# Two heads' scores in two neighbouring PSUM banks under one maximum, with one bank for the up products

## The chip, the cores and the metric

The kernel runs on one core of a Trainium2 chip. The metric is the device time of one execution in microseconds; the median of the runs counts. TensorE (PE) multiplies and transposes into PSUM, which has eight banks of 2 KB per partition; one bank holds one 128x512 float32 result. VectorE (DVE) and ScalarE (ACT) read PSUM, GpSimd (POOL) works in SBUF, and SyncE (SP) issues the DMAs.

## The reference, cut to what matters

Four batches of 512 tokens with 512 features go through four gated layers, each added to its input: a WKV recurrence over time, an FFN with ternary weights and int8 groups, a cross attention with 16 heads, and a ternary linear layer. The change touches the attention and the FFN:

```python
# attention (x is layer-normed; H = 16 heads of Dh = 32)
q = _qdq(x) @ _qdq(wq).T + bq
k, v = jnp.split(cond @ wkv.T + bkv, 2, axis=-1)
attn = jax.nn.softmax(jnp.einsum('bnhd,bmhd->bhnm', q, k) * scale, axis=-1)
o = jnp.einsum('bhnm,bmhd->bnhd', attn, v).reshape(B, N, C)
out = _qdq(o) @ _qdq(wp).T + bp
# FFN (2048 hidden features)
h = jax.nn.silu(_bitlinear(x, w1)) * _bitlinear(x, w2)
return _bitlinear(h, w3)
```

## The kernel before

The four batches are pipelined by hand. Each layer of each batch is a generator; `line(gen, *parts)` gives its steps places on a common axis, where one unit is one FFN and `SLOTS` = 17 slots make one unit; `run(until)` always advances the generator whose next step has the smallest place. Each step is a turn: `in_turn` adds an ordering edge behind the last matmul of the turn before, so PE's order is the order of the turns. The order on the other engines is the tile scheduler's.

After a start-up part (weights, keys and values, WKV and FFN of batch 0) comes what I call the grid: the attention of batch b runs beside the FFN of batch b+1, and for half of each FFN beside the WKV scan of batch b+2 as well. Behind the last FFN the attention of batch 2 is finished, and the attention of batch 3 runs without an FFN (`alone`).

An FFN has 16 units (4 token tiles by 4 blocks of hidden features), of four steps each: an up product of eight matmuls into a bank with tag "hp" (`up`, tile ff_hp), read by a tanh on ACT (L745) and a multiply on DVE (`gate`, L746); the down product of the unit two before (ff_acc, tag "acc"); the second up product, read by one DVE instruction (`gated`, L750) and quantised; and the transposes of the quantised product of the unit before (`gate_parts`, tile tp_ps).

The attention has 16 units as well, of two heads (index i) and two token tiles (index t) each, and two more turns to drain. A unit's four steps, interleaved with those of an FFN unit, are: scores for t = 0; the product with the values of the unit two before (`values`, o_ps) and transposes of the weights of the unit before (`turned`, pt_ps, copied by ACT at L970); scores for t = 1; more transposes, the collection of the results (`collect`), and the fetches on SP's queue. One call of `scores(k, i, t)` makes one matmul into a bank with tag "hp" (s_ps, 128x512), one DVE reduction that gives the negated maximum of each row (at_nm, L948), and one exponential on ACT with that maximum as bias and the row sum as accumulated output (at_P, L950).

PSUM has one pool from the end of the start-up on: three banks with tag "m" (all transposes and projections), three with "hp" (scores and up products), two with "acc". A tile takes a free buffer of its tag; the first instruction that writes a new tile waits until all readers of the buffer's last tile are done.

The functions that the diff touches, and what calls them:

Of the kernel before, what the change touches and what calls it, by code (L numbers as in the profile page):

```python
# [10 lines left out]
F32 = mybir.dt.float32  # L11
# [5 lines left out]
ALU = mybir.AluOpType  # L17
AX = mybir.AxisListType
PSUM = bass.MemoryType.PSUM
DRAM = bass.MemoryType.DRAM  # L20

P = 128
# [8 lines left out]
def kernel(  # L31
# [36 lines left out]
    nc = tc.nc  # L68
    NB, T, D = x.shape
# [11 lines left out]
    sm = ctx.enter_context(tc.tile_pool(name="small", bufs=4))  # L81
# [3 lines left out]
    psum = {}  # L85
# [41 lines left out]
    def psum_tile(name, tag, dtype=F32):  # L127
        pool, bufs = psum["now"]
        return pool.tile([P, D], dtype, name=name, tag=tag, bufs=bufs[tag])
# [17 lines left out]
    def in_turn(ins):  # L147


        if "on" in turn:  # L150
            if "ahead" in turn:
                behind(ins, turn["ahead"])
            turn["last"] = ins
        return ins

    def next_turn():

        if "last" in turn:
            turn["ahead"] = turn["last"]

    def matmul(*args, **kwargs):
        return in_turn(nc.tensor.matmul(*args, **kwargs))  # L162
# [677 lines left out]
    def attention_layer(b, xb, pool, tiles=range(NT)):  # L840
# [41 lines left out]
        qR, kR, V, PT, sums, made, lanes, out_s = {}, {}, {}, {}, {}, {}, {}, {}  # L882
# [38 lines left out]
        def fetch_keys(p):  # L921
            kR[p] = pool.tile([P, 2, T], F32R, name="at_kR", tag="at_kR")
            stack(kR[p], kD[b][p // 2][:, pair(p), :], (0, 1, 0, 1))
# [10 lines left out]

        units = [(p, h) for p in range(NP) for h in range(len(tiles) // 2)]

        def scores(k, i, t):

            p, h = units[k]
            if k not in sums:  # L940
                sums[k] = sm.tile([P, 2, 2], F32, name="at_sum", tag="at_sum")
            at = t * P
            sp = psum_tile("s_ps", "hp")
            matmul(
                sp, lhsT=qR[k][:, i, at : at + P], rhs=kR[p][:, i, :], start=True, stop=True
            )
            nm = sm.tile([P, 1], F32, name="at_nm", tag="at_nm", bufs=8)
            nc.vector.tensor_reduce(nm, sp, AX.X, ALU.max, negate=True)  # L948
            lanes[k, i, t] = pool.tile([P, T], F32, name="at_P", tag="at_P", bufs=6)
            nc.scalar.activation(  # L950
                lanes[k, i, t],
                sp,
                AF.Exp,
                bias=nm,
                accum_out=sums[k][:, t, i : i + 1],
            )

        def turned(k, i, t):

            if k not in PT:  # L960
                PT[k] = pool.tile([P, 2, NT, 2 * P], F32, name="at_PT", tag="at_PT", bufs=1)
            w = lanes.pop((k, i, t))
            pt = psum_tile("pt_ps", "acc" if alone else "m")
            for m in range(NT):
                transpose(pt[:, m * P : (m + 1) * P], w[:, m * P : (m + 1) * P], ident)
            dst = PT[k][:, i, :, t * P : (t + 1) * P]
            if alone and i:
                made[k] = nc.vector.tensor_copy(dst, blocks(pt))
            else:
                made[k] = nc.scalar.copy(dst, blocks(pt))  # L970

        def values(k):


            p, h = units[k]
            acc = bank("o_ps")[:, 0:P]
            for m in range(NT):
                for i in range(2):
                    for t in range(2):
                        mm = matmul(  # L980
                            acc[rows(2 * i + t), :],
                            lhsT=V[p // 2][:, m, rows(2 * (p % 2) + i)],
                            rhs=PT[k][:, i, m, t * P : (t + 1) * P],
                            start=(m == 0),
                            stop=(m == NT - 1),
                        )
                        behind(mm, made[k])
            del PT[k]
            out_s[k] = pool.tile([P, P], F32, name="at_os", tag="at_os", bufs=1)
            nc.scalar.copy(out_s[k], acc)  # L990
# [71 lines left out]
        for k in range(len(units) + 2):  # L1062
            now, before = k < len(units), 0 < k <= len(units)
            if k > 1 and not alone:
                turned(k - 2, 1, 1)
            for i in range(2):
                if now:
                    scores(k, i, 0)
            yield
            if k > 1:  # L1070
                values(k - 2)
            next_turn()
            for i in range(1 + alone):
                if before:
                    turned(k - 1, i, 0)
            if alone and k > len(units):
                next_turn()
                next(ahead)
            yield
            if before and not alone:  # L1080
                turned(k - 1, 1, 0)
            for i in range(2):
                if now:
                    scores(k, i, 1)
            yield
            for i in range(1 + alone):
                if before:
                    turned(k - 1, i, 1)
            next_turn()
            if k > 1:  # L1090
                collect(k - 2)
            if now:
                p, h = units[k]
                if h == 0:
                    if p + 1 < NP:
                        fetch_keys(p + 1)
                    if p % 2 == 0 and p // 2 + 2 < NC:
                        next_turn()
                        project(p // 2 + 2)
                elif p % 2 and p // 2 + 1 < NC:  # L1100
                    fetch_values(p // 2 + 1)
                if k + 2 < len(units):
                    fetch_queries(k + 2)
            yield
# [90 lines left out]
    def place(line):  # L1195

        k = line["step"]
        for start, end, steps in line["parts"]:
            if k < steps:
                at = start + (end - start) * k / steps  # L1200

                return (math.floor(at * SLOTS) + 0.8) / SLOTS if line["aside"] else at
            k -= steps
        return end

    def run(until):
        while lines:
            now = min(lines, key=place)
            if place(now) > until:
                return  # L1210
            try:
                next(now["gen"])
                now["step"] += 1
                next_turn()
            except StopIteration:
                lines.remove(now)

    lines = []

    SLOTS = NT * NF + 1  # L1220

    def line(gen, *parts, aside=False):
        lines.append({"gen": gen, "parts": parts, "step": 0, "aside": aside})

    xs = {}
    with (
# [108 lines left out]
        for b in (2, 3):  # L1335
            line(
                next_batch(b),
                (b - 1.0 - 4.2 / SLOTS, b - 1.0 - 4.2 / SLOTS, 1),
                (b - 1.0 - 3.2 / SLOTS, b - 1.0 - 3.2 / SLOTS, 1),
                (b - 1.0 + 1.8 / SLOTS, b - 1.0 + 5.8 / SLOTS, 4),  # L1340
                (b - 1.0 + 5.05 / SLOTS, b - 1.0 + 13.05 / SLOTS, 32),
            )
        run(0.99)
    nc.sync.dma_start(out=gamma_b, in_=bcast(gamma))
    ps = ctx.enter_context(tc.tile_pool(name="ps", bufs=1, space=PSUM))
    psum["now"] = ps, {"m": 3, "hp": 3, "acc": 2}
    at = ctx.enter_context(tc.tile_pool(name="att", bufs=2))
    for b in range(NB):
        if b:
            early = (0.99, 1.0, 4) if b == 1 else (b - 0.19, b - 0.1, 3), (b - 0.08, b, 1)  # L1350
            line(
                late(lambda b=b: ffn_layer(xs[b])),
                *((early[0],) if b == 1 else early),
                (b, b + 16 / SLOTS, 64),
                (b + 16 / SLOTS, b + 17.75 / SLOTS, 7),
            )
        start = b + 1 + 4.95 / SLOTS
        end = start + 18 / SLOTS
        line(
            late(lambda b=b: attention_layer(b, xs[b], at)),  # L1360
            (b + 1.0 if b == 0 else b + 0.7, b + 1.03 if b == 0 else b + 0.9, 5),
            (b + 1 + 1.7 / SLOTS, b + 1 + 3.7 / SLOTS, 5),
            (b + 1 + 3.75 / SLOTS, b + 1 + 4.35 / SLOTS, 2),
            (start, end, 72),
            (end, end + 2.4 / SLOTS, 6)
            if b != NB - 2
            else (end - 0.15 / SLOTS, end + 4.65 / SLOTS, 6),
            (end + 2.4 / SLOTS, end + 3.4 / SLOTS, 4),
        )
        if b < NB - 1:  # L1370
            line(
                late(lambda b=b: ternary_layer(b, xs[b], at)),
                (end + 3 / SLOTS, end + 8 / SLOTS, 8)
                if b < NB - 2
                else (end + 4.85 / SLOTS, end + 11.85 / SLOTS, 7),
                aside=b < NB - 2,
            )
    run(NB + 9)


# [43 lines left out]
```

## Time and profile before

| what | value |
|---|---|
| median of 3 runs | 1094.46 us (1093.98 to 1096.87) |
| profiled execution | 1094.21 us |
| span of its instructions | 1092.4 us |
| busy PE, DVE, ACT, POOL | 943.3, 827.0, 729.9, 320.7 us |
| granted TensorE clock, mean | 0.956 |
| scores: matmuls, maxima, exponentials | 256 of each |
| up products | 128, of 8 matmuls each |

Times in the lines are microseconds, "mean ns" is the duration of one instruction. "Idle before" is the time in which an engine stood still ahead of an instruction, and "<-" names what ended it. PEld are weight loads, which overlap matmuls. In timelines "x2" means that two neighbouring instructions are merged into one line.

### The profile page before, as it was taken

Reading aid. Unit: us, or ns where it says so; the run is one execution under the profiler, and the core shown is the slowest. Engines: PE = TensorE matmul, PEld = TensorE weight load, DVE = VectorE, ACT = ScalarE, POOL = GpSimd, SP = SyncE. Lnnn points to the kernel's source line nnn. Section 1 sums busy time; section 2 is a strip of 40 time slices with the busy share of each in tenths; the row PEclk is TensorE's granted clock in tenths of the full one; section 3 lists DMA queues with packets and bytes.
Section 4 is the critical chain, followed back from the end, with each engine's and each line's share of the span. In section 5 each row is a group of like instructions: output and inputs, shape, how many; then the busy total and the mean of one; then the engine's idle time right before and its main releaser. Section 6 shows DMA issues by size and latency. Waiting matters only on the chain.

```text
span 1092.4 us, 17928 instructions
## 1 busy us (share of the span) xinstructions
PE 943.3 (86%) x6350; PEld 680.0 (62%) x6380; DVE 827.0 (76%) x1600; ACT 729.9 (67%) x1490; POOL 320.7 (29%) x328
## 2 busy tenths in 40 slices
PE   3879997998879888799997886999999999878975
PEld 2345564565557666677775665677776777655652
DVE  5985548757876899896769898966687866579976
ACT  5656755567545776667877576677685777877863
POOL 3831104423333254621215545412122410100000
PEclk8889999999999999999999798999999999989998
DMA  8188845464445674645576354655574563244311
GB/s 288 39 272 317 323 169 190 144 221 155 154 146 181 221 234 127 231 129 169 185 234 204 121 177 133 204 195 180 184 231 156 184 210 116 59 148 116 116 42 39
DMA packets 85674, 189.68 MB, mean 174 GB/s; under 512 B 12241, under 2 KB 36817, under 8 KB 74577
## 3 DMA queue, kind: packets, MB, share of 16 engines
q1 hardware_dynamic: 85584, 188.53, 51.7%
q8 instruction: 51, 0.84, 0.3%
q14 instruction: 39, 0.31, 0.1%
HBM read 148.65 MB, written 39.85 MB: 173 GB/s over the span
## 4 chain that ended last, share of the span: by engine, by line
PE 49%; DVE 22%; ACT 14%; POOL 5%; issue 5%; DMA 4%; SPq 1%; ACTq 0%; POOLq 0%; DVEq 0%
PE ff_hp L162 15%; PE pt_ps L165 7%; PE ff_acc L162 6%; PE o_ps L162 4%; PE v_ps L162 4%; PE s_ps L162 3%; ACT at_P L950 3%; DVE wk_q L640 3%; ACT at_PT L970 3%; DVE at_nm L948 2%; PE k_ps L162 2%; DVE wk_p L634 1%; PE qr_ps L165 1%; PE tp_ps L165 1%; ACT wk_e L612 1%
## 5 line engine op out<-in xcount | busy, mean ns | idle before, releaser
L162 PE MATMUL ff_hp<-wT,xp 128*128 128x512 f32 x1024 | 275.7, 412 | 6.6 <-DVE ff_z L746 3.7
L162 PEld LDWEIGHTS ff_hp<-wT,xp 128*128 128x128 f32 x1024 | 195.4, 196 | 54.6 <-DVE ff_z L746 5.7
L950 ACT ACTIVATE at_P<-s_ps,at_nm 128x512 f32<-128x512 f32 x256 | 175.0, 690 | 45.2 <-DVE at_nm L948 43.4
L948 DVE TENSOR_REDUCE at_nm<-s_ps 128x1 f32<-128x512 f32 x256 | 166.6, 677 | 38.4 <-PE s_ps L162 37.9
L970 ACT COPY at_PT<-pt_ps 128x512 f32<-128x512 f32 x224 | 131.2, 590 | 72.6 <-PE pt_ps L165 71.9
L685 POOL TENSOR_TENSOR ff_z<-qg_b,qg_s 128x512 f32<-128x512 bf16 x64 | 71.9, 1124 | 314.6 <-ACT qg_b L684 304.7
L165 PE MATMUL pt_ps<-ident,at_P 128*128 128x128 f32 x1024 | 155.4, 280 | 9.0 <-ACT at_PT L970 4.3
L165 PEld LDWEIGHTS pt_ps<-ident,at_P 128*128 128x128 f32 x1024 | 118.1, 142 | 47.3 <-ACT at_PT L970 10.9
L162 PE MATMUL ff_acc<-wT,hr 128*128 128x512 f32 x512 | 137.6, 409 | 5.2 <-DVE hr L697 2.6
L162 PE MATMUL s_ps<-at_kR,at_qR 128*128 128x512 f32 x256 | 103.0, 464 | 24.0 <-ACT at_P L950 17.6
L162 PEld LDWEIGHTS ff_acc<-wT,hr 128*128 128x128 f32 x512 | 92.9, 191 | 26.2 <-DVE hr L697 4.2
L162 PE MATMUL o_ps<-at_PT,at_V 128*32 128x128 f32 x2048 | 75.4, 281 | 4.7 <-ACT at_PT L970 2.8
L162 PEld LDWEIGHTS o_ps<-at_PT,at_V 128*32 128x32 f32 x2048 | 54.8, 111 | 28.6 <-issue 11.6
L746 DVE SCALAR_TENSOR_TENSOR ff_z<-ff_z,ff_hp 128x512 f32<-128x512 f32 x64 | 43.4, 679 | 37.0 <-ACT ff_z L745 36.9
L745 ACT ACTIVATE ff_z<-ff_hp,coef 128x512 f32<-128x512 f32 x64 | 44.1, 688 | 40.5 <-PE ff_hp L162 38.1
L750 DVE SCALAR_TENSOR_TENSOR ff_z<-ff_hp,coef,ff_z 128x512 f32<-128x512 f32 x64 | 47.7, 745 | 30.2 <-PE ff_hp L162 30.1
L684 ACT CAST qg_b<-qg_i 128x512 bf16<-128x512 int8 x80 | 49.3, 617 | 27.4 <-DVE qg_i L680 17.3
L162 PEld LDWEIGHTS s_ps<-at_kR,at_qR 128*128 128x128 f32 x256 | 43.3, 194 | 36.4 <-ACT at_P L950 25.2
L162 PE MATMUL v_ps<-wkvT,cT 128*128 128x512 f32 x128 | 60.5, 618 | 5.5 <-DVE wT L303 2.3
L162 PE MATMUL k_ps<-cT,wkvT 128*128 128x512 f32 x128 | 61.3, 631 | 2.3 <-ACT wk_k L584 1.0
L640 DVE RECIPROCAL wk_q<-wk_q 128x256 f32<-128x256 f32 x32 | 54.5, 1722 | 3.0 <-POOL wk_q L635 1.6
L696 ACT CAST hr<-tp_ps 128x512 fp32r<-128x512 f32 x64 | 37.6, 588 | 21.7 <-PE tp_ps L165 21.7
(180 smaller groups left out, 1669.4 us busy)
## 6 DMA issues: line engine op xcount, KB each, us to landing
wT<-wD SPq DMA_DIRECT2D x72, 1024.0 KB, 5.4
wn<-in_L_ffn_w_dram SPq DMA_DIRECT2D x18, 1024.0 KB, 6.2
at_kR<-kD SPq DMA_DIRECT2D x128, 128.0 KB, 4.0
at_qR<-qD SPq DMA_DIRECT2D x256, 64.0 KB, 2.5
wD<-wT SPq DMA_DIRECT2D x12, 1024.0 KB, 4.2
kD<-k_half SPq DMA_DIRECT2D x16, 512.0 KB, 2.8
qD<-at_half SPq DMA_DIRECT2D x32, 256.0 KB, 2.2
cn<-in_ctx_dram SPq DMA_DIRECT2D x8, 512.0 KB, 5.9
```

Of the source, the lines that this page charges most:

```text
L162: return in_turn(nc.tensor.matmul(*args, **kwargs))
L165: return in_turn(nc.tensor.transpose(*args))
L640: nc.vector.reciprocal(half, half)
L684: nc.scalar.copy(qb, qi)
L685: nc.gpsimd.tensor_tensor(grouped(src), grouped(qb), s.unsqueeze(2).to_broadcast([P, NG, GS]), ALU.mult)
L696: nc.scalar.copy(part[:, 0, :], pt)
L745: nc.scalar.activation(z, hp, AF.Tanh, scale=coef[:, 0:1])
L746: nc.vector.scalar_tensor_tensor(z, z, 1.0, hp, ALU.add, ALU.mult)
L750: nc.vector.scalar_tensor_tensor(z, hp, coef[:, 1:2], z, ALU.mult, ALU.mult)
L948: nc.vector.tensor_reduce(nm, sp, AX.X, ALU.max, negate=True)
L950: nc.scalar.activation(lanes[k, i, t], sp, AF.Exp, bias=nm, accum_out=sums[k][:, t, i : i + 1],)
L970: made[k] = nc.scalar.copy(dst, blocks(pt))
```

## The change

In the grid, the two heads' scores of one token tile go into one PSUM tile of two neighbouring banks (tag "pair", one buffer). One DVE reduction gives both maxima (128x2), and the two exponentials follow. The tag "hp" keeps one bank, which only the up products use in the grid. The pool is closed one slot behind the last FFN, `SWAP` = 1/17 of a unit, and a new pool with the layout of before is opened; from then on scores are made one at a time as before. The start-up part is not touched.

```diff
+        def weighed(k, i, t, sp, nm):
+
             lanes[k, i, t] = pool.tile([P, T], F32, name="at_P", tag="at_P", bufs=6)
             nc.scalar.activation(
                 lanes[k, i, t],
...
-        def scores(k, i, t):
+        def scores(k, t):
 
             p, h = units[k]
             if k not in sums:
                 sums[k] = sm.tile([P, 2, 2], F32, name="at_sum", tag="at_sum")
+            cut = slice(t * P, (t + 1) * P)
+            if "pair" not in psum["now"][1]:
+                for i in range(2):
+                    sp = psum_tile("s_ps", "hp")
+                    matmul(sp, lhsT=qR[k][:, i, cut], rhs=kR[p][:, i, :], start=True, stop=True)
+                    nm = sm.tile([P, 1], F32, name="at_nm", tag="at_nm1", bufs=8)
+                    nc.vector.tensor_reduce(nm, sp, AX.X, ALU.max, negate=True)
+                    weighed(k, i, t, sp, nm)
+                return
+            ps_pool, bufs = psum["now"]
+            sp = ps_pool.tile([P, 2, T], F32, name="s_ps", tag="pair", bufs=bufs["pair"])
+            for i in range(2):
+                matmul(
+                    sp[:, i, :], lhsT=qR[k][:, i, cut], rhs=kR[p][:, i, :], start=True, stop=True
+                )
+            nm = sm.tile([P, 2], F32, name="at_nm", tag="at_nm", bufs=4)
+            nc.vector.tensor_reduce(nm, sp, AX.X, ALU.max, negate=True)
+            for i in range(2):
+                weighed(k, i, t, sp[:, i, :], nm[:, i : i + 1])
...
-            for i in range(2):
-                if now:
-                    scores(k, i, 0)
+            if now:
+                scores(k, 0)
...
-            for i in range(2):
-                if now:
-                    scores(k, i, 1)
+            if now:
+                scores(k, 1)
...
+    SWAP = 1.0 / SLOTS
...
-    ps = ctx.enter_context(tc.tile_pool(name="ps", bufs=1, space=PSUM))
-    psum["now"] = ps, {"m": 3, "hp": 3, "acc": 2}
+    stage = ctx.enter_context(ExitStack())
+    ps = stage.enter_context(tc.tile_pool(name="ps", bufs=1, space=PSUM))
+    psum["now"] = ps, {"m": 3, "hp": 1, "acc": 2, "pair": 1}
...
+    run(NB + SWAP)
+    stage.close()
+    ps = ctx.enter_context(tc.tile_pool(name="ps_end", bufs=1, space=PSUM))
+    psum["now"] = ps, {"m": 3, "hp": 3, "acc": 2}
     run(NB + 9)
```

More of the change, by code (lines that the diff above doesn't have):

```diff
@@ L935, in attention_layer @@
         units = [(p, h) for p in range(NP) for h in range(len(tiles) // 2)]
-        def scores(k, i, t):
[L939 to L948, printed above, removed]
+        def weighed(k, i, t, sp, nm):
             lanes[k, i, t] = pool.tile([P, T], F32, name="at_P", tag="at_P", bufs=6)
@@ L956, in scores @@
             )
+        def scores(k, t):
+            p, h = units[k]
+            if k not in sums:
+                sums[k] = sm.tile([P, 2, 2], F32, name="at_sum", tag="at_sum")
+            cut = slice(t * P, (t + 1) * P)
[17 more added lines that the diff above has]
+                weighed(k, i, t, sp[:, i, :], nm[:, i : i + 1])
         def turned(k, i, t):
```

## The prediction

> **What bounds the kernel now.** I read the page first: PE is busy 86% of the span, DVE 76%, ACT 67%, and the chain that ended last is 49% PE, 22% DVE and 14% ACT. No engine holds the end alone, so I asked for the windows, cut where the grid changes its character. Columns: window, its length, busy time of PE, PEld, DVE, ACT, POOL with instructions, granted clock, DMA share, GB/s.
>
> ```profile
> 365.00:500.00 135.00, 117.59 (x829) 91.28 (x832) 123.44 (x220) 96.56 (x205) 58.45 (x59) 0.96 0.55 175
> 500.00:570.00 70.00, 67.75 (x553) 53.39 (x555) 48.31 (x108) 52.98 (x117) 14.12 (x15) 1.00 0.59 204
> 570.00:690.00 120.00, 95.57 (x636) 72.33 (x633) 106.78 (x186) 80.15 (x161) 63.99 (x61) 0.90 0.52 170
> 690.00:800.00 110.00, 106.39 (x837) 82.81 (x842) 79.50 (x183) 80.42 (x178) 22.47 (x22) 1.00 0.57 186
> ```
>
> The grid (attention of batch b beside the FFN of batch b+1, 365 to 918 us) has two kinds of stretch. Where the WKV scan of a later batch runs too (365 to 500, 570 to 690) DVE is busy 91% and 89% and PE only 87% and 80%: DVE leads. Elsewhere (500 to 570, 690 to 918) PE is busy 96.5% and DVE about 72%: PE leads, and each tenth of a microsecond that PE waits is paid.
>
> Then the costliest groups, for the prices (count, busy us, mean ns, idle before and its releaser):
>
> ```profile
> L950 ACT ACTIVATE at_P<-s_ps,at_nm 128x512 f32<-128x512 f32 x256 | 175.0, 690 | 45.2 <-DVE at_nm L948 43.4
> L948 DVE TENSOR_REDUCE at_nm<-s_ps 128x1 f32<-128x512 f32 x256 | 166.6, 677 | 38.4 <-PE s_ps L162 37.9
> L222 DVE TENSOR_REDUCE w_am<-wn 128x2 f32<-128x1024 f32 x4 | 4.8, 1203 | 3.7 <-DMA wn<-in_L_xattn_wq_dram 3.7
> ```
>
> The third row is the form that the change will issue (two maxima over 2 x 512), though from SBUF. Last, the timeline of one undisturbed unit (start, duration, instruction, idle before):
>
> ```profile
> 519.12 0.71 PE L162 MATMUL s_ps<-at_kR,at_qR 128*128 128x512 f32 x2
> ...
> 519.64 1.29 DVE L948 TENSOR_REDUCE at_nm<-s_ps 128x1 f32<-128x512 f32 x2
> ...
> 520.37 0.69 ACT L950 ACTIVATE at_P<-s_ps,at_nm 128x512 f32<-128x512 f32 x1 [0.38 <-DVE at_nm L948]
> ...
> 521.05 0.68 ACT L950 ACTIVATE at_P<-s_ps,at_nm 128x512 f32<-128x512 f32 x1
> ...
> 522.42 0.72 PE L162 MATMUL s_ps<-at_kR,at_qR 128*128 128x512 f32 x2
> ...
> 522.98 2.00 PE L162 MATMUL ff_hp<-wT,xp 128*128 128x512 f32 x8
> ...
> 525.24 0.68 ACT L745 ACTIVATE ff_z<-ff_hp,coef 128x512 f32<-128x512 f32 x1
> ...
> 526.03 0.69 DVE L746 SCALAR_TENSOR_TENSOR ff_z<-ff_z,ff_hp 128x512 f32<-128x512 f32 x1 [0.52 <-ACT ff_z L745]
> ...
> 527.32 2.01 PE L162 MATMUL ff_hp<-wT,xp 128*128 128x512 f32 x8
> ```
>
> The reader is to see two chains that return to PE: scores, maximum, exponential, next scores; and up product, tanh, multiply, next up product.
>
> **Up products with one bank.** Here the second up product starts at 527.32, after the multiply at 526.03 has let go of the first one's bank (526.72): in the grid the two do not overlap now. I went through all units of the grid: from the 19th unit of the four FFNs (340 us) on, no up product starts before the one ahead of it has been read. Tag "hp" has three buffers and six takers per unit (two scores, an up product, two scores, an up product), so an up product meets the same buffer again and the scores have the other two. The change writes down what the rotation already does, and costs nothing there; the cover is the down product, the values and the transposes that PE has between (up 0 ends 524.98, up 1 starts 527.32). The exception is the first units of batch 1's FFN, before its attention starts. There the second up product starts at 333.66 while the multiply ends at 334.92, the next at 335.57 against 336.52, the next at 337.38 against 339.01: waits of 1.26, 0.95 and 1.63 us, 3.8 together. PE was 90% busy there, so some comes back in later gaps: bounds 0 and 3.8, I take **+2**, the middle.
>
> The Trainium skill ("Perfetto Trace Analysis", section Optimizing Tensor Performance) speaks against one bank: independent matmul groups should rotate through different banks so that reading one overlaps the next group. By the rule every up product would wait for its reading (here 524.98 to 526.72, 1.74 us; 96 of them would be some 167 us); by the row the rotation has stopped overlapping already, and the sum keeps the row.
>
> **One maximum over two banks.** Per pair, two reductions of 677 ns become one of about 1203: 0.15 us of DVE less. If two that stand back to back are the measure (1.29 us above) it is 0.09. The new layout holds until just behind the last FFN: 64 pairs of batches 0 and 1 and 27 of batch 2, 91 in all, so 8.2 to 13.7 us of DVE. Only where DVE leads can it shorten the run: 36 pairs lie in those two windows, 3.2 to 5.4 us; I take **-4.5**, nearer to the row of the same form. Where PE leads, DVE idles anyway. No DMA and nothing on SP or POOL is moved.
>
> **Two exponentials behind one maximum.** Before, the first exponential starts while DVE does the second maximum; the second exponential ends 0.80 us after that maximum (520.93 to 521.73). Now both come behind it: 0.11 for the signal and 0.69 and 0.68, 1.48. So the banks come free 0.68 us later, less the 0.09 to 0.15 that DVE saves: about 0.55; and 0.3 more where DVE stood idle for the second matmul. Queued behind the exponentials on ACT are the tanh, the casts and the copies of the transposed weights.
>
> **One pair buffer.** The next pair's first matmul must now wait for both exponentials, not for one. In the undisturbed unit it starts 0.69 us after the second (521.73 to 522.42), which covers the 0.55 barely. Over the 50 pairs in the stretches that PE leads I compared that matmul's start with the second exponential's end: it comes earlier or less than 0.3 us later eight times (511.64 against 513.21, 530.07 against 530.08, 724.80 against 725.63, 736.74 against 738.28, 755.13 against 755.15, 803.99 against 804.35, 835.35 against 835.88, 865.94 against 865.69). In some of them the second matmul waited already, so what is new is one matmul (0.31) and the 0.55: between 0.2 and 1.4 each, 0.75 in the mean: **+6**, bounds 2 and 11. Where DVE leads the same happens twelve times more, but PE has slack; I take nothing, and up to 36 x 0.5 = 18 us for the upper bound, if the chain of pairs becomes the bound there.
>
> **The tanh behind the exponentials.** Three up products in PE's stretches start 0.05 to 0.61 us after their multiply (752.39, 804.83, 866.57); a tanh that is 0.55 later moves them: **+1.5**, bounds 0 and 2.
>
> **The new PSUM layout.** The pool is closed and opened again once, beside the last batch's start. The profile has one such change, from the start-up pool to this one, near 326 us: there PE stood still 1.30 and 0.72 us in front of the first transposes. If new tiles wait until everything in the old pool is read, PE drains once: **+1.5**, bounds 0 and 4 (one chain of matmul, maximum, two exponentials and the next weights).
>
> **Sum.** 2 - 4.5 + 6 + 1.5 + 1.5 = +6.5 us. The profiled execution took 1094.2 (its span 1092.4 and 1.8 around it), so 1100.7; the median of the runs is 0.25 above it: **1101**. A measurement of this kernel can tell about 0.3%, 3.3 us, from no change.
>
> The skill's same page (Optimizing Scalar/DVE Operations) says both things: larger operations help where the engine is saturated, and breaking them up helps where DVE or ACT is not saturated but makes PE wait. It gives about 125 ns per DVE instruction on PSUM; an estimate by it is 91 x 0.125 = 11.4 us of DVE, inside the bounds above.
>
> **The rivals.**
> *Faster: the DVE time comes through.* If DVE is what the grid waits for even where PE looks full, and a single reduction spares the pairs whose second maximum now stands far behind the first (376.83 and 383.47, with 1.23 and 1.78 us of WKV between), the saving is up to 13.7 and the waits are covered: 1081 to 1091, middle 1087. For it: the chain gives DVE 22%, and 35.8 us of ACT idle in the grid end with this maximum. Against: PE at 96.5% over half the grid. It decides if the waits that I price at 9.5 are below 1.
> *No change.* The buffers were divided so already, and savings and waits cancel: 1094.5 within 3.3.
> *Much slower: the pair's chain becomes the bound where DVE leads.* A 1.2 us reduction behind a WKV reciprocal of 1.7 us holds both banks; 18 us on top of the rest: 1112 to 1125. For it: PE waits up to 2.2 us for these exponentials there. Against: two turns of about 3.6 us each (0.7 + 1.2 + 1.4 and signals) in a unit of some 12 us.
>
> **How the numbers follow.** Forecast (1098 to 1112) 0.45; faster 0.27; no change 0.16; much slower 0.12. Slower is 0.45 + 0.12 = 0.57. The range for 8 in 10 takes the upper two thirds of the faster case and the lower third of the much slower one: 1084 to 1117. The forecast's own range is 1098 to 1112.
>
> **What would show it.** Right: the reduction with 128x2 near 1.2 us, 91 times; DVE busy 8 to 14 us less; PE's waits for the exponentials in the grid above the present 8.5 us; a gap of 1 to 3 us near the second layout; the 500 to 570 stretch a little longer and the 365 to 500 stretch a little shorter. Wrong: PE's waits unchanged, or the 690 to 800 stretch shorter, or up products waiting for their bank all through the grid.

## The result, and the profile after

The kernel became slower: 1124.12 us (median of 4 runs, 1123.95 to 1124.5) against 1094.39 (4 runs, 1093.98 to 1096.87) on the same chip, ratio 1.0267 [1.0249, 1.0285]. Slower was the likeliest forecast, but with 6.6 us in place of 29.7, and the time lies above the range.

The profiled execution after has a span of 1122.2 us, 29.8 more than before, at nearly the same mean granted clock (0.955 against 0.956). PE is busy 946.0 us (before 943.3), DVE 828.9 (827.0), ACT 726.1 (729.9). So no engine has got much more to do; PE stands still 27.1 us longer. The groups say in front of what (count, busy us, mean ns, idle before and its releasers). PE's rows before:

```profile
L162 PE MATMUL ff_hp<-wT,xp 128*128 128x512 f32 x1024 | 275.7, 412 | 6.6 <-DVE ff_z L746 3.7 <-ACT at_P L950 2.1 <-DVE xp L697 0.7
...
L162 PE MATMUL s_ps<-at_kR,at_qR 128*128 128x512 f32 x256 | 103.0, 464 | 24.0 <-ACT at_P L950 17.6 <-DMA at_qR<-qD 4.2 <-DVE ff_z L746 1.8
```

and the rows after:

```profile
L162 PE MATMUL ff_hp<-wT,xp 128*128 128x512 f32 x1024 | 277.4, 413 | 13.8 <-DVE ff_z L746 11.9 <-DVE ff_z L750 1.3 <-DVE xp L697 0.7
...
L940 ACT ACTIVATE at_P<-s_ps,at_nm 128x512 f32<-128x512 f32 x256 | 174.6, 689 | 68.4 <-DVE at_nm L969 57.8 <-DVE at_nm L959 5.4 <-DVE at_s L226 3.6
...
L969 DVE TENSOR_REDUCE at_nm<-s_ps 128x2 f32<-128x1024 f32 x91 | 110.0, 1209 | 36.4 <-PE s_ps L162 36.1
L162 PE MATMUL s_ps<-at_kR,at_qR 128*128 128x512 f32 x256 | 100.0, 460 | 44.5 <-ACT at_P L940 40.7 <-DMA at_qR<-qD 3.8
```

PE's idle time was 24.0 us ahead of the scores (17.6 of it released by an exponential) and 6.6 ahead of the up products. Now it is 44.5 (40.7) and 13.8: 20.5 + 7.2 = 27.7 us more, where PE's whole idle time grew by 27.1; the other rows changed by little together. The scores' wait for the exponentials is the largest part. The merged reduction takes 1209 ns, 91 times; ACT stands still 57.8 us for it and 5.4 for the single ones that remain, where the single ones of before made it wait 43.4.

To see where it arose, I took the start of the first up product of chosen units (of the 64 that four FFNs have, numbered from 0) in both traces, and the start and end of batch 3's attention; each row is the growth of the difference in that stretch, in us. The other columns are experiments described below, each against the profile before.

| stretch | after | e6 | e5 | e8 | e10 |
|---|---|---|---|---|---|
| first units of batch 1's FFN | 4.1 | 4.2 | 4.1 | 4.1 | 0.4 |
| units 21 to 31, DVE leads | 7.1 | 2.1 | 4.2 | 9.0 | 1.0 |
| between the FFNs of batches 1 and 2 | 3.4 | 0.6 | 3.2 | 3.8 | 2.8 |
| units 32 to 47, DVE leads in the first part | 3.3 | 0.1 | -1.2 | -1.8 | 2.1 |
| between the FFNs of batches 2 and 3 | 3.2 | 1.0 | 2.6 | 3.0 | 2.0 |
| units 48 to 63, PE leads | 4.4 | 1.1 | 4.7 | 5.1 | 6.0 |
| behind the last up products, to batch 3's first scores | 5.7 | 2.9 | 7.3 | 8.1 | 5.4 |
| the rest | -1.4 | 0.8 | 0.4 | -0.5 | -1.0 |
| span | 29.8 | 12.8 | 25.3 | 30.8 | 18.7 |

A wide loss, then, in seven places. Some views show its kinds. First the start, in the timeline after (start, duration, engine, instruction, idle before):

```profile
334.48 2.11 PE L162 MATMUL ff_hp<-wT,xp 128*128 128x512 f32 x8 [1.07 <-DVE ff_z L746]
...
337.43 2.14 PE L162 MATMUL ff_hp<-wT,xp 128*128 128x512 f32 x8 [0.84 <-DVE ff_z L750]
...
341.28 2.12 PE L162 MATMUL ff_hp<-wT,xp 128*128 128x512 f32 x8 [1.72 <-DVE ff_z L746]
```

Three up products wait for the reader of the one ahead, as the prediction had it. Next, windows cut at the same up products: before, from unit 21 to unit 31 and from there to unit 32 (window, length, busy PE, PEld, DVE, ACT, POOL, clock, DMA share, GB/s),

```profile
365.63:494.50 128.87, 111.56 (x773) 86.49 (x774) 117.61 (x207) 90.92 (x193) 57.82 (x58) 0.96 0.57 179
494.50:513.36 18.86, 17.83 (x152) 13.70 (x150) 15.37 (x33) 14.86 (x36) 3.63 (x3) 1.00 0.45 157
```

and after:

```profile
369.47:505.39 135.92, 112.40 (x773) 87.51 (x774) 116.09 (x185) 89.92 (x194) 58.27 (x58) 0.95 0.55 172
505.39:527.62 22.23, 17.91 (x151) 13.91 (x150) 16.01 (x30) 15.64 (x36) 3.13 (x3) 1.00 0.53 183
```

In the first pair of lines DVE does save 1.5 us, but its share falls from 91% to 85%: it stands still 8.6 us longer. In the second pair PE does the same 17.9 us of work in 3.4 us more. The waits of PE in the first stretch (total us, times, longest), before,

```profile
PE s_ps L162 <- ACT at_P L950: 6.5, 4, 2.2
PE ff_hp L162 <- DVE ff_z L746: 3.7, 1, 3.7
...
PE ff_acc L162 <- DVE hr L697: 1.0, 2, 0.6
```

and after,

```profile
PE s_ps L162 <- ACT at_P L940: 9.7, 5, 2.7
PE ff_hp L162 <- DVE ff_z L746: 5.5, 3, 2.6
PE ff_acc L162 <- DVE hr L697: 3.1, 2, 1.9
```

show that the loss there is spread: scores 3.2 more, up products 1.8, down products 2.1. My reading, which no run tests, is that where scores start late, what DVE does behind them is late as well. The second stretch is the slot between two FFNs. There PE has no up product to put between two pairs; in the timeline after:

```profile
522.53 0.73 PE L162 MATMUL s_ps<-at_kR,at_qR 128*128 128x512 f32 x2
...
523.12 0.69 DVE L191 BATCH_NORM_STATS2 s<-xb 128x6 f32<-128x512 f32 x1
...
523.74 1.21 DVE L969 TENSOR_REDUCE at_nm<-s_ps 128x2 f32<-128x1024 f32 x1
...
525.07 0.59 ACT L985 COPY at_PT<-pt_ps 128x512 f32<-128x512 f32 x1 [0.20 <-PE pt_ps L165]
...
525.55 0.69 ACT L940 ACTIVATE at_P<-s_ps,at_nm 128x512 f32<-128x512 f32 x1
...
527.05 0.73 PE L162 MATMUL s_ps<-at_kR,at_qR 128*128 128x512 f32 x2 [2.02 <-ACT at_P L940]
```

From scores to scores this is 4.52 us: the maximum ended at 524.95, a copy held ACT until 525.66, and PE stood still 2.02 us. The same slot before:

```profile
510.18 0.71 PE L162 MATMUL s_ps<-at_kR,at_qR 128*128 128x512 f32 x2
...
510.70 1.29 DVE L948 TENSOR_REDUCE at_nm<-s_ps 128x1 f32<-128x512 f32 x2
...
511.64 0.47 PE L162 MATMUL s_ps<-at_kR,at_qR 128*128 128x512 f32 x1
...
511.85 0.69 ACT L950 ACTIVATE at_P<-s_ps,at_nm 128x512 f32<-128x512 f32 x1
...
512.76 0.68 DVE L191 BATCH_NORM_STATS2 s<-xb 128x6 f32<-128x512 f32 x1
```

The next pair's first scores came 1.46 us behind these: with no up product in the slot, the scores had all three "hp" banks. The order on the other engines was also different. Before, the statistic (512.76), a cast (513.19) and a copy (513.65) stood behind this pair's maxima and exponentials; after, all three stand ahead of them. So the change does not only make instructions wait, it also makes the scheduler order them anew: of ACT's 1198 instructions (accumulator reads left out) 93 stand in another order in the trace after, of DVE's 1344 without the maxima 145.

Last, the end. Behind the last up products the first product with the values in the new pool waits for the last exponential of the old one, in the timeline after:

```profile
966.51 1.72 PE L162 MATMUL o_ps<-at_PT,at_V 128*32 128x128 f32 x28 [4.35 <-ACT at_P L940]
```

### The profile page after: what moved, and what is told of

It reads as the page before. It is cut to its first block, busy times and chain, and to the rows that moved or that the text cites. A ratio compares the mean times of both kernels' runs of the same rounds, so it can differ in the third digit from the quotient of the medians.

```text
span 1122.2 us, 17891 instructions
## 1 busy us (share of the span) xinstructions
PE 946.0 (84%) x6350; PEld 683.1 (61%) x6380; DVE 828.9 (74%) x1509; ACT 726.1 (65%) x1490; POOL 321.9 (29%) x328
## 5 line engine op out<-in xcount | busy, mean ns | idle before, releaser
L162 PE MATMUL ff_hp<-wT,xp 128*128 128x512 f32 x1024 | 277.4, 413 | 13.8 <-DVE ff_z L746 11.9
L940 ACT ACTIVATE at_P<-s_ps,at_nm 128x512 f32<-128x512 f32 x256 | 174.6, 689 | 68.4 <-DVE at_nm L969 57.8
L162 PE MATMUL s_ps<-at_kR,at_qR 128*128 128x512 f32 x256 | 100.0, 460 | 44.5 <-ACT at_P L940 40.7
L969 DVE TENSOR_REDUCE at_nm<-s_ps 128x2 f32<-128x1024 f32 x91 | 110.0, 1209 | 36.4 <-PE s_ps L162 36.1
L162 PEld LDWEIGHTS o_ps<-at_PT,at_V 128*32 128x32 f32 x2048 | 54.5, 111 | 30.8 <-issue 13.1
L750 DVE SCALAR_TENSOR_TENSOR ff_z<-ff_hp,coef,ff_z 128x512 f32<-128x512 f32 x64 | 47.7, 745 | 33.0 <-PE ff_hp L162 32.8
L959 DVE TENSOR_REDUCE at_nm<-s_ps 128x1 f32<-128x512 f32 x74 | 48.4, 682 | 13.9 <-PE s_ps L162 13.7
```

The lines of the kernel that those rows point to most:

```text
L750: nc.vector.scalar_tensor_tensor(z, hp, coef[:, 1:2], z, ALU.mult, ALU.mult)
L940: nc.scalar.activation(lanes[k, i, t], sp, AF.Exp, bias=nm, accum_out=sums[k][:, t, i : i + 1],)
```

## The experiments

"Before" was run on the same chip beside each; e10, e13 and e14 ran on another chip than the rest (before 1094.09 us there).

**e1: the division alone.** Single banks and single maxima, divided between the uses as after.

```diff
-    psum["now"] = ps, {"m": 3, "hp": 1, "acc": 2, "pair": 1}
+    psum["now"] = ps, {"m": 3, "hp": 1, "acc": 2, "s": 2}
-                    sp = psum_tile("s_ps", "hp")
+                    sp = psum_tile("s_ps", "s" if "s" in psum["now"][1] else "hp")
```

> The changed kernel's division of the banks (up products one, scores two, with the second layout behind the last FFN), but the scores in single banks, each with its own maximum, as before. Theory T1 (what costs is that the two banks of a pair come free together, only behind the second exponential): most of the 30 us comes back, 1097 to 1104, that is +3 for the second layout and up to +6 for the first units of batch 1's FFN. Rival T2 (the fixed division costs: up products and scores can no longer borrow each other's bank): 1110 to 1124, with the WKV stretch 365 to 500 us and the ends of the FFNs as long as in the changed kernel. My own reading of the trace after: +4 at the first units of batch 1's FFN stays whichever theory holds.

1099.81 us (10 runs, 1094.75 to 1103.9) against 1094.9, ratio 1.0044 [1.0026, 1.0062]: 4.9 us. Its profiled execution was the quickest of the ten, so its trace understates that; it shows 4.1 in the first units of batch 1's FFN, 2.6 behind the last up products, and up to 3.4 less in other stretches. Its times go with the granted clock: 1094.75 and 1095.36 us at 0.966, 1103.73 and 1103.9 at 0.952. In its groups the scores' wait for exponentials is near that before (17.6):

```profile
L162 PE MATMUL s_ps<-at_kR,at_qR 128*128 128x512 f32 x256 | 103.5, 463 | 26.0 <-ACT at_P L940 20.9 <-DMA at_qR<-qD 4.7
```

So the loss is not the division of the banks; some 25 us come with the pair.

**e2: the pair's tile with two maxima.**

```diff
-            nm = sm.tile([P, 2], F32, name="at_nm", tag="at_nm", bufs=4)
-            nc.vector.tensor_reduce(nm, sp, AX.X, ALU.max, negate=True)
             for i in range(2):
-                weighed(k, i, t, sp[:, i, :], nm[:, i : i + 1])
+                nm = sm.tile([P, 1], F32, name="at_nm", tag="at_nm1", bufs=8)
+                nc.vector.tensor_reduce(nm, sp[:, i, :], AX.X, ALU.max, negate=True)
+                weighed(k, i, t, sp[:, i, :], nm)
```

> The changed kernel with its pair tile of two banks, but with two reductions of 512 in place of one of 1024, so that the first exponential can start as early as before. T1 (banks released together): stays slow, 1117 to 1127, since the tile is still free only behind the second exponential. Rival T3 (one late maximum delays the first exponential and all that is queued on ACT behind it): 1100 to 1110. In DVE time: 91 x 0.15 = 14 us more than the changed kernel.

1143.21 us (1138.72 to 1146.52, 4 runs), ratio 1.0431 [1.0403, 1.046]: slower than after by 19, and above both expectations. The group of e2's maxima, and then its timeline, say why:

```profile
L970 DVE TENSOR_REDUCE at_nm<-s_ps 128x1 f32<-128x512 f32 x182 | 123.9, 681 | 76.5 <-PE s_ps L162 43.9 <-ACT at_P L940 31.6
```

```profile
519.29 0.69 ACT L940 ACTIVATE at_P<-s_ps,at_nm 128x512 f32<-128x512 f32 x1 [1.08 <-DVE at_nm L970]
...
520.10 0.69 DVE L970 TENSOR_REDUCE at_nm<-s_ps 128x1 f32<-128x512 f32 x1 [0.84 <-ACT at_P L940]
```

The second maximum starts when the first exponential has ended, though it reads another bank: in this program two engines take turns on one tile. So e2 put in a wait of its own and did not measure lateness; e5 to e8 replace it with single tiles and explicit waits.

**e3: the new pool alone.** After's program, with the layout of before on both sides of the new pool, so that scores are single all through.

```diff
-    psum["now"] = ps, {"m": 3, "hp": 1, "acc": 2, "pair": 1}
+    psum["now"] = ps, {"m": 3, "hp": 3, "acc": 2}
```

> The kernel before with nothing but the closing and opening of the pool one slot behind the last FFN, the same layout (3, 3, 2) on both sides. T4 (the new pool waits until the old one is read): 1097 to 1099, +3 to +4.4 as the trace after shows at 969.86 us against 936.60 before. If tiles only wait for the tiles whose place they take: 1094.4, no difference within 3.

1094.13 us (10 runs, 1092.02 to 1098.71), ratio 0.9995 [0.9981, 1.0008]. Closing and opening the pool costs nothing that the medians can show. Its profile has 2.0 us in the stretch behind the last up products, and -2.3 over all others. The 2.0 have their place in its timeline, where after has its 4.35:

```profile
934.57 1.41 PE L162 MATMUL o_ps<-at_PT,at_V 128*32 128x128 f32 x32 [2.00 <-ACT at_P L940]
```

Before waits for no exponential ahead of such a product, but 1.58 us for one ahead of the next scores (940.11); e1 and e7 wait 1.59 in e3's place, e6 2.03, e5 3.90 and e8 4.40. So the new pool does hold PE, longer where the exponentials are late.

**e4: a second bank for the up products,** taken from the transposes.

```diff
-    psum["now"] = ps, {"m": 3, "hp": 1, "acc": 2, "pair": 1}
+    psum["now"] = ps, {"m": 2, "hp": 2, "acc": 2, "pair": 1}
```

> The changed kernel with two banks for the up products and two instead of three for the transposes and projections. If the single up bank is a main cost (T2's half): the first units of batch 1's FFN lose no 4 us and the WKV stretch shortens by 5 or more, 1108 to 1116, less what the missing transpose bank costs. T1: the pair tile still holds, 1116 to 1126. If the third transpose bank matters more than either: over 1126.

1158.88 us (1157.42 to 1161.16, 4 runs), ratio 1.0579 [1.0563, 1.0595]: 35 us slower than after. The start's loss is gone (0.5 in place of 4.1 up to its third unit), so the one bank was its cause. But two banks for the transposes are too few. A wait of e4 (total us, times, longest):

```profile
PEld tp_ps L165 <- issue: 38.5, 51, 2.3
```

After has 12.3 us in this row.

**e5, e6, e8: the two properties of a pair, one at a time.** On e1's banks, `awaits` adds a wait of one instruction for another. In e5 the first maximum waits for the second matmul and the first exponential for the second maximum: both exponentials are late, but each bank is still released by its own. In e6 nothing is late, but the first matmul of the next pair waits for the second exponential. e8 has both, so it is the change with two reductions in place of one.

```diff
+                for i in range(2):
+                    sps.append(psum_tile("s_ps", "s" if split else "hp"))
+                    mms.append(
+                        matmul(sps[i], lhsT=qR[k][:, i, cut], rhs=kR[p][:, i, :], start=True, stop=True)
+                    )
+                if split and "e" in last_exp:
+                    awaits(mms[0], last_exp["e"])          # e6, e8
+                for i in range(2):
...
+                    reds.append(nc.vector.tensor_reduce(nms[i], sps[i], AX.X, ALU.max, negate=True))
+                if split:
+                    awaits(reds[0], mms[1])                # e5, e8
                 for i in range(2):
+                    e = weighed(k, i, t, sps[i], nms[i])
+                    if split and i == 0:
+                        awaits(e, reds[1])                 # e5, e8
+                last_exp["e"] = e
```

> Single banks as in e1, with two added waits that copy the lateness of the one maximum: the first reduction waits for both matmuls, the first exponential for both reductions. Each bank still comes free by itself. If the lateness is what costs (T3): 20 us or more over e1, 1115 to 1125. If it is the release of both banks together (T1): 1100 to 1108.

> Single banks as in e1, with one added wait: a pair's first matmul waits for the second exponential of the pair before, as in the tile of two banks. Maxima and exponentials as early as before. T1: 1112 to 1124. T3: 1100 to 1106. By the trace of before, counting only the waits that the rows show (7.5 us over the grid), 1104 to 1110.

> Both sets of added waits, of e5 and e6: the changed kernel's dependencies with two reductions in place of one. If these two, and nothing about the tile itself, are the cause: at or somewhat above the changed kernel, 1122 to 1135 (91 x 0.09 to 0.15 us of DVE more). If something else in the tile costs: clearly below, 1105 to 1115.

| | median us (range, runs) | ratio to before | above e1 | scores' wait for exponentials, above e1 |
|---|---|---|---|---|
| e6, joint release | 1106.94 (1105.03 to 1107.43, 4) | 1.011 [1.0097, 1.0123] | 7.1 | 7.7 |
| e5, late exponentials | 1115.1 (1111.4 to 1119.46, 4) | 1.0189 [1.0165, 1.0213] | 15.3 | 14.1 |
| e8, both | 1126.47 (1123.18 to 1131.48, 4) | 1.0301 [1.0274, 1.0328] | 26.7 | 22.0 |
| after | 1124.12 | 1.0267 [1.0249, 1.0285] | 24.3 | 19.8 |

The last column is from the group of the scores' matmuls in each trace; e6, e5 and e8 in turn:

```profile
L172 PE MATMUL s_ps<-at_kR,at_qR 128*128 128x512 f32 x256 | 101.9, 465 | 33.9 <-ACT at_P L950 28.6 <-DMA at_qR<-qD 5.1
```

```profile
L172 PE MATMUL s_ps<-at_kR,at_qR 128*128 128x512 f32 x256 | 107.3, 470 | 40.3 <-ACT at_P L950 35.0 <-DMA at_qR<-qD 4.9
```

```profile
L172 PE MATMUL s_ps<-at_kR,at_qR 128*128 128x512 f32 x256 | 100.8, 462 | 47.7 <-ACT at_P L950 42.9 <-DMA at_qR<-qD 4.3
```

The time grows with the wait, in this order of the four, though the traces are not of the median runs (e1's is its quickest, e5's its slowest). Neither theory holds alone: the late exponentials cost about twice the joint release. That the two together cost more than their sum (22.4) is not clear of the scatter, which is 8 us in e5 and in e8 and 9 in e1. Part of the scatter goes with the granted clock: at 0.952 e1 took 1103.7 to 1103.9 us and e6 1106.9 to 1107.0, so the joint release alone may be nearer to 3 than to 7. e8 reproduces the change to 2.4 us, and in the table of stretches to 2.4 or less, except for units 32 to 47 (5.1).

What e5 does not separate is the added wait from the order that the scheduler makes because of it. Against e1, 111 of ACT's 1198 instructions stand in another order in e5, and 23 in e6. No run holds the order fixed, so how much of the 15.3 us is waiting as such stays open.

**e13: which of e5's two waits.** e5 without the first maximum's wait for the second matmul.

```diff
-                if split:
-                    awaits(reds[0], mms[1])
```

> e5 without the first of its two waits: the first reduction starts as soon as its own matmul is done, only the first exponential waits for both reductions. If the wait of ACT for the second maximum is the cost: 1111 to 1118, as e5. If the 0.3 us that DVE waits for the second matmul is a good part of it: 1101 to 1108.

1119.49 us (1116.63 to 1126.65, 4 runs), ratio 1.0251 [1.0212, 1.029]: no cheaper than e5. The wait of the first exponential for the second maximum, with the order made for it, is what costs.

**e10: lateness in the layout of before.** Three "hp" banks shared by scores and up products, e5's waits in the attentions of batches 0 to 2. Against e5:

```diff
-    psum["now"] = ps, {"m": 3, "hp": 1, "acc": 2, "s": 2}
+    psum["now"] = ps, {"m": 3, "hp": 3, "acc": 2}
-                split = "s" in psum["now"][1]
+                split = not alone
...
-                    sps.append(psum_tile("s_ps", "s" if split else "hp"))
+                    sps.append(psum_tile("s_ps", "hp"))
```

> The lateness of e5 alone (first reduction waits for both matmuls, first exponential for both reductions), but in the layout of the kernel before, where scores and up products share three banks. e5 cost 15 us over e1, and its trace puts some 10 of them where an FFN has no up products (the slots between two FFNs and the end of the last one). If the spare third bank covers the lateness there: 1099 to 1105, +5 to +10 over the kernel before. If the lateness costs the same with any layout: 1108 to 1114.

1112.86 us (1112.36 to 1112.93, 4 runs), ratio 1.0168 [1.015, 1.0185]: 18.8 us. Lateness costs about as much without the fixed division. The wait has another name in part; in the groups of e10 the scores wait 10.7 us for the DVE instruction that reads the second up product (L760, before L750), whose bank they now meet:

```profile
L172 PE MATMUL s_ps<-at_kR,at_qR 128*128 128x512 f32 x256 | 102.8, 464 | 32.7 <-ACT at_P L950 16.9 <-DVE ff_z L760 10.7 <-DMA at_qR<-qD 4.8
```

Against before (17.6 and 1.8) this is 8.2 us more, not half of the 18.8; the rest is spread over rows that I did not settle.

**e7: the start mended.** On e1, the second up product of the first five units of batch 1's FFN takes a score bank, since that batch's scores have not begun.

```diff
-            hp = psum_tile("ff_hp", "hp")
+            hp = psum_tile("ff_hp", "s" if i and units.index((t, f)) < free else "hp")
-                late(lambda b=b: ffn_layer(xs[b])),
+                late(lambda b=b: ffn_layer(xs[b], free=5 if b == 1 else 0)),
```

> e1 with one edit: in the first five units of batch 1's FFN, beside which no attention runs yet, the second up product takes one of the two idle score banks. If the 4.1 us that e1 and the changed kernel lose between the first and the third of these units come from the single up bank, and are not given back later: 4 us below e1, 1091 to 1096, at or below the kernel before. If later gaps had taken them back anyway: as e1.

1097.22 us (12 runs, 1092.66 to 1099.54), ratio 1.0016 [1.0003, 1.003]. The start loses 0.1 in place of 4.1. In the timeline of e7 three up products now run as one stretch:

```profile
333.54 5.74 PE L162 MATMUL ff_hp<-wT,xp 128*128 128x512 f32 x24
```

The time is 2.6 us below e1's, between the two expectations: about half of the 4.9 us, with intervals that overlap. It does not beat the kernel before; in its trace 2.9 us arise behind the last up products, where the new pool is opened.

**e14: the opposite direction.** If late maxima and exponentials are so dear, earlier ones might pay. Before, with the scheduler told to prefer both.

```diff
-            nc.vector.tensor_reduce(nm, sp, AX.X, ALU.max, negate=True)
+            with tc.high_priority(60):
+                nc.vector.tensor_reduce(nm, sp, AX.X, ALU.max, negate=True)
...
+            with tc.high_priority(60):
+                nc.scalar.activation(
```

> The kernel before, with its maxima and exponentials given priority by 60 instructions in the scheduler's order, so that on DVE and ACT they stand ahead of the WKV scan and the quantisation that come before them in the program. If lateness of the exponentials costs 15 us, earliness should gain, most where DVE leads: 1084 to 1092. If what is put behind them (tanh, up products' multiplies) is as urgent: 1093 to 1105.

1113.19 us (1112.57 to 1116.29, 4 runs), ratio 1.0177 [1.0155, 1.0199]: slower, not faster, and above both expectations. The scores' wait did shrink, but others grew, as the groups of e14 show:

```profile
L162 PE MATMUL ff_acc<-wT,hr 128*128 128x512 f32 x512 | 138.8, 412 | 11.1 <-ACT hr L696 7.5 <-DVE hr L697 3.6
...
L162 PE MATMUL s_ps<-at_kR,at_qR 128*128 128x512 f32 x256 | 103.6, 469 | 16.9 <-ACT at_P L952 13.0 <-DMA at_qR<-qD 3.9
```

Down products now wait 7.5 us for ACT's share of the quantised product (2.6 before), and 7.5 of the loss arose in units 21 to 31, 11.7 around batch 3's attention. So a smaller wait in one row is no gain by itself. No wait was added here, only the scheduler's preference was changed (146 of ACT's 1198 instructions stand in another order). So a new order can cost as much as e5's 15.3 us without an added wait, and it stays a rival there.

## Why the prediction was wrong

The sign was right, and so was the mechanism of the largest term: scores that wait for later exponentials. Its size was wrong, because the prediction let only eight pairs pay and none where DVE leads; and the -4.5 for DVE had the wrong sign for its stretch.

**"One pair buffer" and "Two exponentials behind one maximum": forecast +6, bounds 2 and 11.** I counted the pairs in PE's stretches in which the old slack was under 0.3 us, eight of fifty, and priced each at 0.75. Three of the eight (511.64, 724.80, 736.74) lie in the slots between two FFNs, where scores ran ahead into a third bank; the end behind the last up products I did not count at all. The lateness itself was priced well. Over the 91 pairs the second exponential ended 1.17 us behind the last maximum in the mean before (0.80 in the median) and 1.92 after (1.50, where the prediction had 1.48), and from the first matmul to that end a pair took 4.42 and now 4.93 us, so 0.51 longer. What failed is who pays: between 365 us and the last up products PE waited for an exponential ahead of scores 18 times, 28.9 us in all (`--waits`, to 945 us), where it was 7 times and 8.5 us before (to 917 us). The table after puts 3.4, 3.2 and 5.7 us on the two slots and the end behind the last up products, and 4.4 on units 48 to 63: 16.7, with nothing of units 32 to 47. In the 5.7 stands the wait of 4.35 behind the new pool. In a slot the price was too low because I let one matmul and 0.55 us be late, while there the whole turn from scores to scores comes to lie on PE: 4.52 us instead of 1.46. And the turn was not the 3.6 us that I added up from durations: a statistic on DVE and a copy on ACT stood inside it, which had stood behind it before. The prediction took the order on DVE and ACT as given. e6 and e5 give the two parts as 7.1 and 15.3 over the whole kernel. The sign that I had named for it, waits for the exponentials in the grid above 8.5 us, came.

**"Where DVE leads ... PE has slack; I take nothing" and the -4.5.** Units 21 to 31 got 7.1 us longer, not some 3 shorter. A busy share of 91% did not make DVE the limit: it stood still 8.6 us longer and its share fell to 85%. These waits are spread over many rows; the one for the scores grew from 2.0 to 3.9 us. The upper bound of 18 was the right kind of caution, and the rival "much slower" held the time (1112 to 1125), but its place was wrong: at most 10.4 of the 29.8 us (units 21 to 47) lie where it put them.

**The DVE saving of 8 to 14 us.** The reductions fell from 166.6 us to 110.0 + 48.4 (74 single ones remain), 8.2. DVE's busy time did not fall: other operations took longer in total, the quantising step (qg_i, L680) 46.4 to 49.7 and the scan's wk_p 29.4 to 32.1 among them. What the merged reduction brings to the time is the difference of 2.4 us between e8 and after; their intervals overlap, so it may be nothing.

**The start: +2, bounds 0 and 3.8.** It cost 4.1 in its stretch, just over the upper bound; of this e7, which loses 0.1 there, gives back 2.6. The rest of "up products with one bank" held: e7 is 2.6 us above before, so the division costs little elsewhere. The Trainium skill ("Perfetto Trace Analysis", Optimizing Tensor Performance) would have independent matmul groups rotate through banks; the runs agree at the start (e7). In the grid no run tests it alone: there the rotation of before had already stopped overlapping, so the division took nothing away.

**The new layout: +1.5, bounds 0 and 4.** Without a pair it is free by the medians (e3), though PE waits 2.00 us behind it. In the kernel after PE waits 4.35 there, just over the upper bound, since the exponentials that it waits for are late. **The tanh: +1.5.** Not visible as a term of its own: the up products' added 7.2 us of waiting hold the start's 4.1 and the 1.8 of units 21 to 31.

Of the skill's two rules on DVE and ACT work (same page, Optimizing Scalar/DVE Operations), the second fits what happened: breaking instructions up may let work complete sooner where these engines are not saturated but make others wait. e5 measures the reverse step, with the order made for it, at 15.3 us. The first, that grouping can help a saturated engine, brought no shorter stretch even where DVE was busy 91%.

In sum, 1094.6 to 1124.1 is: some 5 us for the division with its second pool; some 22 to 27 for the joint release and the late exponentials, the late exponentials the larger part; and perhaps 2 back from the merged reduction. The parts are differences of medians, each uncertain by 2 to 4 us.

## What to carry to other kernels

Merging two short instructions also merges what they wait for and what they release. Before pricing the saving, write down the whole turn of the buffers (here matmul, maximum, exponential, next matmul) with everything that its engines' queues hold in between, and look for the places where nothing else covers it, such as the seams between two layers. A high busy share of an engine does not show that less work for it shortens the stretch: ask whether its inputs come later. Where a scheduler orders the engines, look at the order too: a new dependency can move other instructions ahead of the late one.

## What the runs showed that I had not expected

- Two engines' accesses to different banks of one tile took turns: 31.6 us of DVE waiting in e2. That is how this program was ordered; whether the banks themselves would allow it at once was not tried.
- The third bank for transposes is worth 35 us or more here (e4 against after, 34.8 us, even though e4 got 3.6 of the start's 4.1 back).
- One reduction over 1024 elements took 1209 ns from PSUM, two of 512 took 677 each: 0.15 us saved per pair by these durations, 0.09 by DVE's busy time (8.2 us over 91), against a turn between two FFNs that grew by 3.1.
- Preferring the urgent instructions cost 19.1 us (e14) although the wait it aimed at shrank from 17.6 to 13.0 us. Why the schedule gets so much worse was not settled.
